# Decays of two groups of a quad in SBUF, the next decays in mid-step, and four smaller edits in a Mamba and convolution kernel

## The chip, the cores and the metric

The kernel runs on one core of one Trainium2 chip. The time is that of the device in microseconds (us), from the first to the last instruction and what lies around them; a kernel is measured several times and the median counts. A core has a matrix engine (TensorE, called PE), a vector engine (VectorE, DVE), an activation engine (ScalarE, ACT), a general engine (GpSimd, POOL) and a queue that issues transfers (SyncE, SP). Each takes its own instructions in the order in which they were written; semaphores tie the engines together. SBUF is the working memory; PSUM, eight banks of 128 x 512 float32, takes the results of matmuls, and POOL works in SBUF alone here.

## The reference

Four layers follow one another on x (8 images, 384 channels, 32 x 32 pixels, float32). Each normalises its input in 32 groups of channels and adds its result to it. Layer 0 is a Mamba block, layer 1 a spectral filter with a gated convolution, layer 2 a Mamba block with layer norm and an MLP, layer 3 a 3 x 3 depthwise convolution.

```python
def _mamba(xseq, ...):
    xin, z = jnp.split(xseq @ in_proj_w.T, 2, axis=-1)
    u = silu(conv1d_depthwise(xin, conv_w) + conv_b)
    dbc = u @ x_proj_w.T
    dt, Bm, Cm = dbc[..., :24], dbc[..., 24:40], dbc[..., 40:]
    dt = softplus(dt @ dt_proj_w.T + dt_proj_b)
    A = -jnp.exp(A_log)

    def step(h, inp):
        dt_t, B_t, C_t, u_t = inp
        dA = jnp.exp(dt_t[..., None] * A)
        h = dA * h + (dt_t * u_t)[..., None] * B_t[:, None, :]
        y = jnp.einsum('bdn,bn->bd', h, C_t)
        return (h, y)
    ...
    y = y + u * D
    return (y * silu(z)) @ out_proj_w.T
...
x = x + L0(_gn(x))
x = x + L1(_gn(x))
x = x + L2(_gn(x))
x = x + L3(_gn(x))
```

There are 768 inner channels with 16 states each, and 1024 positions in an image. The recurrence over positions, h = dA * h + dt*u*B, is the bulk of the work.

## The kernel before

**Tiling.** Each image is cut into two chunks of T = 512 positions, so 16 chunks of layer 0 and 16 of layer 2. A chunk's 768 channels times 16 states are 96 tiles of 128 rows by 512 positions. Four such tiles (groups 0 to 3) make a quad, and one quad is one step: 24 steps a chunk (6 blocks k of 128 channels, 4 quads `sub` in each), 768 steps in all. The recurrence is one DVE scan instruction per group.

**A step t of the main loop**, in the order in which its instructions are issued:

1. `times` of step t+1 (L623): POOL multiplies the four groups of g, which hold dt*u, by B, in two products of two groups each.
2. `scan` of step t (L643 to L660): for groups 0 and 1, DVE scans in place in the PSUM bank `dA[j]`, and multiplies by C into g (L654); for groups 2 and 3 the scan reads the bank and writes g, and POOL multiplies both by C in one product (L660). In the first chunk of an image the last column goes to `carry` (L653 from PSUM, L656 from SBUF).
3. Filler: up to 2 us of matmul work of other jobs (`jobs.step(t, 2.0)`).
4. `gather` of step t-1: matmuls that sum over states into the PSUM tile y; after the fourth quad of a block, u*D is added (a matmul by the diagonal matrix `w_D` in layer 0, a DVE instruction in layer 2) and DVE multiplies by the gate.
5. `begin` of step t+3: SP's transfer that spreads dt*u (`dud` in HBM) over g, after `jobs.until` has forced that chunk's `dud` to be there.
6. Filler: as much of other jobs as the room of this step allows (`jobs.step(t)`).
7. `decay` of step t+1: four matmuls put dt on the four banks `dA[0..3]`, and ACT takes exp(A * dt) of each in place.

PSUM's eight banks are the four `dA`, one y and three (`ps`) that all other work shares.

**Other work.** Everything else is a list of jobs, Python generators that go on piece by piece. `front` prepares the next chunk (normalise, project, convolve, u, then per block d `step_dt`: softplus into dt, POOL's dt*u into a tile du, four transfers of it to `dud`). `gates` makes the gate z of half a chunk; `measure` takes the statistics of a later image; `finish` does the output projection and, in layer 2, the MLP; `layer1` and `layer3` run once per image. Each has a first and a last step; the one due first goes first. `Jobs.step` lets a piece run when its matmul and vector costs fit the room left in this step (5.2 and 3.0 us in layer 0, 6.4 and 3.0 in layer 2). `Jobs.until(done)` is the exception: it runs pieces of all jobs, in order of due time, until a wanted thing is there. It is called at steps 4 and 16 of a chunk for the gates, and before `begin` for `dud`.

**SBUF tiles of the front.** The tag `spm` has two buffers, used by the softplus, by `measure`'s loads and by the layer norm's squares; `live["spm"]` says that `measure` holds them. `du` has two buffers, `dt` has seven (`NDT`).

Of the kernel before, what the change touches and what calls it, by code (L numbers as in the profile page):

```python
# [16 lines left out]
P = 128  # L17
# [72 lines left out]
class Jobs:  # L90
# [56 lines left out]

    def until(self, done):

        while not done():  # L150
            if not any(self.piece(job) for job in self.in_order()):
                raise RuntimeError("no job goes on")
# [3 lines left out]
def tile_conv_preact_d4(ctx: ExitStack, tc: tile.TileContext, a: dict, out: bass.AP):  # L156
# [9 lines left out]

    live = {"ps": 0, "dt": 0, "x": 0, "spm": False}
    work = [0.0, 0.0]
# [186 lines left out]

    def load_diagonal(w, pre):
        w["D"] = wk.tile([P, ND, P], F32, tag="w_D", name="w_D")
        nc.sync.dma_start(w["D"], a[pre + "D"].rearrange("d p q -> p d q"))

    def load_out(w, pre):  # L360
# [38 lines left out]
    def measure(s):  # L399

        blocks = [(h, k) for h in range(2) for k in range(KC)]
        loaded = {}

        def load(q):
            if q < len(blocks):
                h, k = blocks[q]
                x = loaded[h, k] = wk.tile([P, T], F32, tag="spm", name="xk", bufs=2)
                nc.sync.dma_start(
                    x, s["src"][s["b"], k * P : (k + 1) * P, h * T : (h + 1) * T]
                )  # L410

        live["spm"] = True
        load(0)
        load(1)
        yield NEXT

        def block(h, k):
            return loaded.pop((h, k)), lambda: load(blocks.index((h, k)) + 2)

        def all_read():  # L420
            live["spm"] = False

        s["stats"] = yield from group_stats(block, all_read, NEXT)
# [36 lines left out]
    def layer_norm(xn):  # L460
        ps = yield from ps_tile("ps_ln")
        for k in range(KC):
            mm(ps, ln_mean, xn[:, k, :], start=k == 0, stop=k == KC - 1)
        for k in range(KC):
            vector.tensor_sub(xn[:, k, :], xn[:, k, :], ps)
        ps_done()
        yield NEXT
        while live["spm"]:
            yield WAIT
        ps = yield from ps_tile("ps_lv")  # L470
        for k in range(KC):
            sq = wk.tile([P, T], F32, tag="spm", name="sq", bufs=2)
            act(sq, xn[:, k, :], AF.Square)
            mm(ps, ln_mean, sq, start=k == 0, stop=k == KC - 1)
        rsqrt(ps, ps, eps_ln)
        yield
        for k in range(KC):
            vector.scalar_tensor_tensor(
                xn[:, k, :], xn[:, k, :], ln_w[:, k : k + 1], ps, ALU.mult, ALU.mult
            )  # L480
        ps_done()
        yield NEXT
        for k in range(KC):
            act(xn[:, k, :], xn[:, k, :], AF.Identity, bias=ln_b[:, k : k + 1])
        yield NEXT

    def front(s):

        c, n = s["c"], s["n"]
        while n > 0 and ("gates", 1) not in chunks[n - 1]:  # L490
            yield WAIT
# [56 lines left out]
        exp_again()  # L548
        yield NEXT
        ps = yield from ps_tile("ps_x")  # L550
        for d in range(ND):
# [14 lines left out]
        def step_dt(d):  # L566
            got = {}


            def log(ps):  # L570
                mm(ps, w["dt"][DT0:RX, d * P : (d + 1) * P], dbc[DT0:RX, :])
                v = got["m"] = wk.tile([P, T], F32, tag="spm", name="spm", bufs=2)
                act(v, ps, AF.Abs)
                act(v, v, AF.Exp, scale=-1.0)
                act(v, v, AF.Ln, bias=1.0)

            def plus(ps):
                v = s["dt"][d] = wk.tile([P, T], F32, tag="dt", name="dt", bufs=NDT)
                vector.scalar_tensor_tensor(v, ps, 0.0, got["m"], ALU.max, ALU.add)

            def times_u(ps):
                v = got["du"] = wk.tile([P, T], F32, tag="du", name="du", bufs=2)
                nc.gpsimd.tensor_mul(v, s["dt"][d], u[d])

            def spill(ps):
                to = s["dud"][d] = dram.tile(
                    [NSUB * E8, 4, T], F32, tag="dud", name="dud", bufs=2 * ND
                )
                for j in range(4):
                    nc.sync.dma_start(to[:, j, :], got["du"][32 * j : 32 * (j + 1), :])  # L590

            return [both(log, plus), None, both(times_u, spill)]

        yield from pipe([("ps_bc", [spread(j)]) for j in range(2)])
        yield
        flying = []
        for d in range(ND):
            while live["dt"] >= NDT or live["spm"]:
                yield WAIT
            live["dt"] += 1  # L600

            flying.append(pipe([("ps_dt", step_dt(d))]))
            flying = [f for f in flying if next(f, f) is not f]
            yield NEXT
        while flying:
            flying = [f for f in flying if next(f, f) is not f]
            yield NEXT

# [18 lines left out]
    def decay(s, i):  # L627
# [4 lines left out]
        if sub == NSUB - 1:  # L632
            live["dt"] -= 1
        for j in range(4):
            act(dAs[j], dAs[j], AF.Exp, scale=s["w"]["A"][:, 4 * i + j : 4 * i + j + 1])

    def scan(s, i):
# [3 lines left out]
        for j in range(4):  # L641
            q = 4 * i + j
            nc.vector.tensor_tensor_scan(  # L643
                dAs[j] if j < own else g[:, j, :],
                dAs[j],
                g[:, j, :],
# [17 lines left out]
    def gather(s, i):  # L664
# [6 lines left out]
        for j in range(4):  # L671
            mm(y[32 * j : 32 * (j + 1), :], sely[:, sub, :], g[:, j, :], sub == 0, sub == NSUB - 1 and s["pre"] == "l2_")
        if sub == NSUB - 1:
            u = s["u"][k // NH][:, k % NH, :]
            if s["pre"] == "l0_":
                mm(y, s["w"]["D"][:, k, :], u, start=False)
            else:
                nc.vector.scalar_tensor_tensor(
                    y, u, s["w"]["vec"][:, k, 4:5], y, ALU.mult, ALU.add
                )  # L680
# [326 lines left out]
    jobs.until(lambda: ("gates", 0) in chunks[0])  # L1007
    load_diagonal(layer_w["l0_"], "l0_")
    jobs.until(lambda: not jobs.jobs)
# [3 lines left out]
    times(*steps[0])  # L1013
    decay(*steps[0])
    for t in range(total):
        s, i = steps[t]
        n = s["n"]
        later = chunks[n + 1] if n + 1 < len(chunks) else None
        if i == 0:
            jobs.add("gates", gates(s, 1), t + 1, t + 8)  # L1020
            if s["c"] == 0 and n + NCH < len(chunks):
                jobs.add("measure", measure(chunks[n + NCH]), t, t + NQ + 4)
            if later:
                jobs.add("front%d" % (later["pre"] == "l2_"), front(later), t + 3, t + 14)
                jobs.add("gates", gates(later, 0), t + 13, t + NQ + 2)
        if i % (NH * NSUB) == NSUB:
            jobs.until(lambda: ("gates", i // (NH * NSUB)) in s)
        if t + 1 < total:
# [10 lines left out]
        if t + AHEAD < total:  # L1039
            p, q = steps[t + AHEAD]  # L1040
            jobs.until(lambda: p.get("dud", {}).get(QUADS[q][0]))
            begin(p, q)
        jobs.step(t)
        if t + 1 < total:
            decay(*steps[t + 1])
    gather(*steps[-1])
# [132 lines left out]
```

## Time and profile before

| what | value |
|---|---|
| median of 3 runs | 7789.29 us (7782.02 to 7790.03) |
| the profiled execution | 7774.96 us, span 7773.2 us |
| granted TensorE clock, mean | 0.922 |
| first scan to first scan of layer 2 | 95.1 to 3552.3 us: 384 steps |
| first scan of layer 2 to POOL's last product | 3552.3 to about 7590 us: 384 steps |

A line of the profile's groups names the source line, engine and operation, then what is written and read with its shape and the count; behind the bar stand the busy time in us and the mean of one in ns, then the idle time of the engine just before these instructions and what ended most of it. Most calls go through helpers, so L177 is any matmul, L241 any activation and L85 most of DVE's work outside the scan; the names of the tiles tell them apart. In a table of waits a line reads: who waited, for whom, us in total, times, longest. In a table of stretches it reads: start and end, length, busy us of each engine with its instructions, granted clock, share of the DMA engines and GB/s. A timeline's line has the start, the length, the engine and the instruction; neighbours of one kind are merged into one line with their count.

### The profile page before, as it was taken

Reading aid. Unit: us, or ns where it says so; the run is one execution under the profiler, and the core shown is the slowest. Engines: PE = TensorE matmul, PEld = TensorE weight load, DVE = VectorE, ACT = ScalarE, POOL = GpSimd, SP = SyncE. Lnnn points to the kernel's source line nnn. Section 1 sums busy time; section 2 is a strip of 40 time slices with the busy share of each in tenths; the row PEclk is TensorE's granted clock in tenths of the full one; section 3 lists DMA queues with packets and bytes.
Section 4 is the critical chain, followed back from the end, with each engine's and each line's share of the span. In section 5 each row is a group of like instructions: output and inputs, shape, how many; then the busy total and the mean of one; then the engine's idle time right before and its main releaser. Section 6 shows DMA issues by size and latency. Waiting matters only on the chain. (4 is left out here: it accounts for less than half of the span.)

```text
span 7773.2 us, 76689 instructions
## 1 busy us (share of the span) xinstructions
PE 7244.1 (93%) x25762; PEld 3001.0 (39%) x25762; DVE 5787.0 (74%) x7350; ACT 4034.0 (52%) x6980; POOL 5638.8 (73%) x2710
## 2 busy tenths in 40 slices
PE   7989999999999999999999989999999999999998
PEld 2223333333333333333334434444444444444445
DVE  5988788888777878778746765767777677776871
ACT  4445555554554555455545544555555555555543
POOL 5888878788787878778646764767767677676770
PEclk8888889999888999988899999999999999999999
DMA  5666556556565646556536654666656666565662
GB/s 141 141 151 144 138 134 142 136 135 150 127 146 127 141 120 148 128 139 146 129 78 167 174 135 120 165 156 172 165 150 174 155 170 164 149 164 146 171 168 67
DMA packets 288919, 1122.50 MB, mean 144 GB/s; under 512 B 37386, under 2 KB 90970, under 8 KB 190220
## 3 DMA queue, kind: packets, MB, share of 16 engines
q1 hardware_dynamic: 288524, 1117.59, 58.4%
q8 instruction: 204, 3.34, 0.2%
q14 instruction: 191, 1.56, 0.1%
HBM read 1041.96 MB, written 75.50 MB: 144 GB/s over the span
## 5 line engine op out<-in xcount | busy, mean ns | idle before, releaser
L623 POOL TENSOR_TENSOR g<-g,bc 128x1024 f32<-128x1024 f32 x1536 | 3586.8, 2358 | 197.2 <-DMA g<-dud 181.2
L660 POOL TENSOR_TENSOR g<-g,bc 128x1024 f32<-128x1024 f32 x768 | 1806.2, 2352 | 1441.1 <-DVE carry L656 806.6
L241 ACT ACTIVATE dA<-dA,w_A 128x512 f32<-128x512 f32 x3072 | 1860.7, 662 | 1543.3 <-PE dA L177 1530.1
L177 PE MATMUL dA<-dt,selr 32*128 32x512 f32 x6144 | 1573.3, 677 | 70.6 <-DVE g L654 61.9
L643 DVE TENSOR_TENSOR_SCAN dA<-dA,carry,g 128x512 f32<-128x512 f32 x768 | 986.6, 1285 | 616.0 <-issue 275.6
L643 DVE TENSOR_TENSOR_SCAN dA<-dA,g 128x512 f32<-128x512 f32 x768 | 940.6, 1225 | 477.5 <-issue 167.7
L654 DVE TENSOR_TENSOR g<-dA,bc 128x512 f32<-128x512 f32 x1536 | 1053.9, 686 | 29.8 <-DVE dA L643 0.5
L177 PE MATMUL y<-g,sely 128*32 128x512 f32 x6144 | 934.1, 637 | 43.0 <-POOL g L660 37.5
L643 DVE TENSOR_TENSOR_SCAN g<-dA,carry,g 128x512 f32<-128x512 f32 x768 | 940.6, 1267 | 0.0
L643 DVE TENSOR_TENSOR_SCAN g<-dA,g 128x512 f32<-128x512 f32 x768 | 893.3, 1204 | 0.0
L177 PEld LDWEIGHTS dA<-dt,selr 32*128 32x128 f32 x6144 | 470.2, 191 | 984.4 <-DVE g L643 517.3
L177 PE MATMUL ps_dn<-h,mw 128*128 128x256 f32 x2304 | 573.9, 401 | 75.3 <-DMA mw<-in_l_mlp_w 58.6
L177 PE MATMUL ps_up<-t,mw 128*128 128x256 f32 x2304 | 566.8, 394 | 59.0 <-DMA mw<-in_l_mlp_w 44.2
L177 PE MATMUL ps_z<-xf,w_in 128*128 128x512 f32 x1152 | 586.1, 649 | 27.3 <-DVE dt L85 23.6
L177 PE MATMUL ps_in<-xf,w_in 128*128 128x512 f32 x1152 | 566.9, 633 | 27.3 <-DVE u L85 25.5
L177 PE MATMUL ps_dw<-tp,diag 96*96 96x512 f32 x1152 | 572.8, 638 | 15.2 <-ACT diag L241 15.2
L177 PE MATMUL ps_out<-u,w_out 128*128 128x512 f32 x1152 | 543.7, 619 | 10.2 <-DVE x L85 10.2
L177 PEld LDWEIGHTS ps_dn<-h,mw 128*128 128x128 f32 x2304 | 439.5, 197 | 277.0 <-issue 118.8
L177 PEld LDWEIGHTS ps_up<-t,mw 128*128 128x128 f32 x2304 | 425.8, 192 | 268.4 <-issue 148.9
L177 PE MATMUL ps_dw<-xp,diag 128*128 128x512 f32 x864 | 407.5, 622 | 42.2 <-ACT diag L241 40.9
L241 ACT ACTIVATE u<-ps_in,w_vec 128x512 f32<-128x512 f32 x192 | 149.4, 778 | 484.2 <-PE ps_in L177 484.2
L177 PEld LDWEIGHTS y<-g,sely 128*32 128x32 f32 x6144 | 134.2, 111 | 648.5 <-issue 461.1
(99 smaller groups left out, 6463.1 us busy)
## 6 DMA issues: line engine op xcount, KB each, us to landing
g<-dud SPq DMA_DIRECT2D x768, 1024.0 KB, 7.1
mw<-in_l_mlp_w SPq DMA_DIRECT2D x384, 384.0 KB, 7.4
dud<-du SPq DMA_DIRECT2D x768, 64.0 KB, 1.7
xk<-in_x SPq DMA_DIRECT2D x48, 256.0 KB, 4.2
xf<-in_x SPq DMA_DIRECT2D x16, 768.0 KB, 8.4
x<-in_x SPq DMA_DIRECT2D x16, 768.0 KB, 8.5
x_mid<-x SPq DMA_DIRECT2D x16, 768.0 KB, 4.6
xk<-x_mid SPq DMA_DIRECT2D x48, 256.0 KB, 5.0
```

What stands on the lines that cost most here:

```text
L177: nc.tensor.matmul(out_, lhsT, rhs, start=start, stop=stop)
L241: nc.scalar.activation(out_, in_, func, **kw)
L623: nc.gpsimd.tensor_mul(g, g, s["bc"][:, 0, :].unsqueeze(1).to_broadcast([P, 2, T]))
L643: nc.vector.tensor_tensor_scan(dAs[j] if j < own else g[:, j, :], dAs[j], g[:, j, :], 0.0 if s["c"] == 0 else carry[:, q : q + 1], ALU.mul ...
L654: nc.vector.tensor_mul(g[:, j, :], dAs[j], s["bc"][:, 1, :])
L660: nc.gpsimd.tensor_mul(g, g, s["bc"][:, 1, :].unsqueeze(1).to_broadcast([P, 4 - own, T]))
```

## The change

Six edits come together.

- The exponentials of groups 2 and 3 write SBUF tiles e2 and e3 (one buffer each) instead of their PSUM banks; scans 2 and 3 read them there. They are split off into `decay_out`.
- `decay` (four matmuls, two exponentials in place) is issued before the second filler; `decay_out` (two exponentials) stays behind it.
- dt*u is written over the softplus tile, so `du` goes; `spm` has three buffers. `live["spm"]` now names who holds them, and `front`'s loop over blocks waits for it, and goes on with blocks under way while the next one has to wait.
- The diagonal matrix of D is made by ACT from the identity, one block at a time, instead of being loaded whole.
- The layer norm's three squares are taken a piece ahead of their matmuls.
- `until` can be given a sort of job, which it then tries first; the gates of the two halves become two sorts, and those of the first half are due at step 20 instead of 26. Two further waits in `front` keep the order of buffers.

```diff
-    def until(self, done):
+    def until(self, done, kind=None):
         while not done():
-            if not any(self.piece(job) for job in self.in_order()):
+            late = [job for job in self.in_order() if job["kind"] == kind]
+            if not any(self.piece(job) for job in late + self.in_order()):
                 raise RuntimeError("no job goes on")
...
+        live["spm"] = "squares"
+        sq = [wk.tile([P, T], F32, tag="spm", name="sq", bufs=3) for _ in range(KC)]
+        for k in range(KC):
+            act(sq[k], xn[:, k, :], AF.Square)
+        yield NEXT
         ps = yield from ps_tile("ps_lv")
         for k in range(KC):
-            sq = wk.tile([P, T], F32, tag="spm", name="sq", bufs=2)
-            act(sq, xn[:, k, :], AF.Square)
-            mm(ps, ln_mean, sq, start=k == 0, stop=k == KC - 1)
+            mm(ps, ln_mean, sq[k], start=k == 0, stop=k == KC - 1)
+        live["spm"] = None
...
+        while n > 0 and "spread" not in chunks[n - 1]:
+            yield WAIT
         ps = yield from ps_tile("ps_x")
...
-                v = got["m"] = wk.tile([P, T], F32, tag="spm", name="spm", bufs=2)
+                v = got["m"] = wk.tile([P, T], F32, tag="spm", name="spm", bufs=3)
...
             def times_u(ps):
-                v = got["du"] = wk.tile([P, T], F32, tag="du", name="du", bufs=2)
-                nc.gpsimd.tensor_mul(v, s["dt"][d], u[d])
+                nc.gpsimd.tensor_mul(got["m"], s["dt"][d], u[d])
...
-        flying = []
-        for d in range(ND):
-            while live["dt"] >= NDT or live["spm"]:
-                yield WAIT
-            live["dt"] += 1
-            flying.append(pipe([("ps_dt", step_dt(d))]))
+        flying, d = [], 0
+        while d < ND or flying:
+            went = bool(flying)
+            if d < ND and live["dt"] < NDT and live["spm"] in (None, "dt"):
+                went = True
+                live["dt"] += 1
+                live["spm"] = "dt"
+                flying.append(pipe([("ps_dt", step_dt(d))]))
+                d += 1
             flying = [f for f in flying if next(f, f) is not f]
-            yield NEXT
-        while flying:
-            flying = [f for f in flying if next(f, f) is not f]
-            yield NEXT
+            if went and not flying:
+                live["spm"] = None
+            yield NEXT if went else WAIT
+        s["spread"] = True
...
-        for j in range(4):
+        for j in range(2):
             act(dAs[j], dAs[j], AF.Exp, scale=s["w"]["A"][:, 4 * i + j : 4 * i + j + 1])
+
+    def decay_out(s, i):
+        s["e"] = []
+        for j in range(2, 4):
+            e = wk.tile([P, T], F32, tag="e%d" % j, name="e%d" % j)
+            act(e, dAs[j], AF.Exp, scale=s["w"]["A"][:, 4 * i + j : 4 * i + j + 1])
+            s["e"].append(e)
...
                 dAs[j] if j < own else g[:, j, :],
-                dAs[j],
+                dAs[j] if j < 2 else s["e"][j - 2],
                 g[:, j, :],
...
+        if sub == NSUB - 2 and s["pre"] == "l0_":
+            s["D", k] = wk.tile([P, P], F32, tag="D", name="D")
+            act(s["D", k], eye, AF.Copy, scale=s["w"]["vec"][:, k, 4:5])
...
-                mm(y, s["w"]["D"][:, k, :], u, start=False)
+                mm(y, s.pop(("D", k)), u, start=False)
...
-                jobs.add("gates", gates(later, 0), t + 13, t + NQ + 2)
+                jobs.add("gates0", gates(later, 0), t + 13, t + NQ - 4)
         if i % (NH * NSUB) == NSUB:
-            jobs.until(lambda: ("gates", i // (NH * NSUB)) in s)
+            h = i // (NH * NSUB)
+            jobs.until(lambda: ("gates", h) in s, "gates%d" % h)
...
             begin(p, q)
+        if t + 1 < total:
+            decay(*steps[t + 1])
         jobs.step(t)
         if t + 1 < total:
-            decay(*steps[t + 1])
+            decay_out(*steps[t + 1])
```

More of the change, by code (lines that the diff above doesn't have):

```diff
@@ L165, in tile_conv_preact_d4 @@
     psy = ctx.enter_context(tc.tile_pool(name="psy", bufs=1, space=PSUM))
-    live = {"ps": 0, "dt": 0, "x": 0, "spm": False}
+    live = {"ps": 0, "dt": 0, "x": 0, "spm": None}
     work = [0.0, 0.0]
@@ L354, in load_mamba @@
         return w
-    def load_diagonal(w, pre):
-        w["D"] = wk.tile([P, ND, P], F32, tag="w_D", name="w_D")
-        nc.sync.dma_start(w["D"], a[pre + "D"].rearrange("d p q -> p d q"))
     def load_out(w, pre):
@@ L406, in load @@
                 h, k = blocks[q]
-                x = loaded[h, k] = wk.tile([P, T], F32, tag="spm", name="xk", bufs=2)
+                x = loaded[h, k] = wk.tile([P, T], F32, tag="spm", name="xk", bufs=3)
                 nc.sync.dma_start(
@@ L410, in load @@
                 )
-        live["spm"] = True
+        while live["spm"]:
+            yield WAIT
+        live["spm"] = "measure"
         load(0)
@@ L420, in all_read @@
         def all_read():
-            live["spm"] = False
+            live["spm"] = None
         s["stats"] = yield from group_stats(block, all_read, NEXT)
@@ L489, in front @@
         c, n = s["c"], s["n"]
-        while n > 0 and ("gates", 1) not in chunks[n - 1]:
+        while n > 0 and ("gates", 1) not in chunks[n - 1] or "stats" not in chunks[n - c]:
             yield WAIT
@@ L549, in front @@
         yield NEXT
+        while n > 0 and "spread" not in chunks[n - 1]:
+            yield WAIT
         ps = yield from ps_tile("ps_x")
@@ L589, in spill @@
                 for j in range(4):
-                    nc.sync.dma_start(to[:, j, :], got["du"][32 * j : 32 * (j + 1), :])
+                    nc.sync.dma_start(to[:, j, :], got["m"][32 * j : 32 * (j + 1), :])
             return [both(log, plus), None, both(times_u, spill)]
@@ L595, in front @@
         yield
-        flying = []
-        for d in range(ND):
-            while live["dt"] >= NDT or live["spm"]:
-                yield WAIT
-            live["dt"] += 1
-            flying.append(pipe([("ps_dt", step_dt(d))]))
+        flying, d = [], 0
[7 more added lines that the diff above has]
+                d += 1
             flying = [f for f in flying if next(f, f) is not f]
-            yield NEXT
-        while flying:
-            flying = [f for f in flying if next(f, f) is not f]
-            yield NEXT
+            if went and not flying:
+                live["spm"] = None
+            yield NEXT if went else WAIT
+        s["spread"] = True
     def begin(s, i):
@@ L1007, in tile_conv_preact_d4 @@
     jobs.until(lambda: ("gates", 0) in chunks[0])
-    load_diagonal(layer_w["l0_"], "l0_")
     jobs.until(lambda: not jobs.jobs)
@@ L1014, in tile_conv_preact_d4 @@
     decay(*steps[0])
+    decay_out(*steps[0])
     for t in range(total):
@@ L1019, in tile_conv_preact_d4 @@
         if i == 0:
-            jobs.add("gates", gates(s, 1), t + 1, t + 8)
+            jobs.add("gates1", gates(s, 1), t + 1, t + 8)
             if s["c"] == 0 and n + NCH < len(chunks):
@@ L1040, in tile_conv_preact_d4 @@
             p, q = steps[t + AHEAD]
-            jobs.until(lambda: p.get("dud", {}).get(QUADS[q][0]))
+            jobs.until(
+                lambda: p.get("dud", {}).get(QUADS[q][0]), "front%d" % (p["pre"] == "l2_")
+            )
             begin(p, q)
+        if t + 1 < total:
+            decay(*steps[t + 1])
         jobs.step(t)
         if t + 1 < total:
-            decay(*steps[t + 1])
+            decay_out(*steps[t + 1])
     gather(*steps[-1])
```

## The prediction, made before the changed kernel was run

> **What bounds the kernel now.** I read the page's engine shares and costliest groups first, then the waits, then the stretches, then two timelines. The groups that carry the argument, with the line of engine totals:
>
> ```profile
> PE 7244.1 (93%) x25762; PEld 3001.0 (39%) x25762; DVE 5787.0 (74%) x7350; ACT 4034.0 (52%) x6980; POOL 5638.8 (73%) x2710
> ...
> L623 POOL TENSOR_TENSOR g<-g,bc 128x1024 f32<-128x1024 f32 x1536 | 3586.8, 2358 | 197.2 <-DMA g<-dud 181.2
> L660 POOL TENSOR_TENSOR g<-g,bc 128x1024 f32<-128x1024 f32 x768 | 1806.2, 2352 | 1441.1 <-DVE carry L656 806.6
> ...
> L643 DVE TENSOR_TENSOR_SCAN g<-dA,carry,g 128x512 f32<-128x512 f32 x768 | 940.6, 1267 | 0.0
> L643 DVE TENSOR_TENSOR_SCAN g<-dA,g 128x512 f32<-128x512 f32 x768 | 893.3, 1204 | 0.0
> ```
>
> PE's 93% includes matmuls held back by waits, so I don't take it as a roof. Per step (768 of them), DVE is busy 5787.0/768 = 7.54 us and POOL 5638.8/768 = 7.34 us, in a step of about 9.8 us. No engine is full; the step is set by a loop through engines, which the waits show:
>
> ```profile
> ACT dA L241 <- PE dA L177: 1530.1, 847, 16.2
> ...
> PEld dA L177 <- DVE g L643: 517.3, 740, 1.7
> ...
> DVE dA L643 <- issue: 443.3, 237, 9.5
> DVE dA L643 <- ACT dA L241: 286.8, 129, 8.4
> ```
>
> PE waits for groups 2 and 3 of the last scan before it may refill their banks, ACT waits for PE, and DVE waits for ACT at the head of a step ("issue" there too: the first scan starts within a microsecond of the exponentials). This is what the change attacks. Its sum by stage (start, layer 0, layer 2, tail; PE, PEld, DVE, ACT, POOL busy):
>
> ```profile
> 0.00:95.00 95.00, 54.42 (x120) 23.36 (x120) 18.58 (x32) 36.65 (x56) 14.77 (x16) 0.83 0.47 134
> 95.00:3552.00 3457.00, 3265.38 (x10785) 1132.41 (x10786) 2839.33 (x3566) 1816.76 (x3220) 2814.61 (x1350) 0.90 0.58 138
> 3552.00:7590.00 4038.00, 3763.95 (x14345) 1744.64 (x14344) 2914.75 (x3727) 2123.17 (x3584) 2808.26 (x1342) 0.95 0.61 153
> 7590.00:7773.00 183.00, 160.37 (x515) 100.58 (x513) 14.38 (x26) 57.41 (x120) 1.13 (x5) 0.92 0.22 69
> ```
>
> So a step takes 3457/384 = 9.00 us in layer 0 and 4038/384 = 10.52 in layer 2, where POOL idles 4038 - 2808 = 1230 us, partly in bursts in which forced matmuls run and the scans stand still.
>
> The decisive lines are DVE's and POOL's timelines of one step:
>
> ```profile
> 274.77 2.33 DVE L643 TENSOR_TENSOR_SCAN g<-dA,g 128x512 f32<-128x512 f32 x2
> 277.13 2.36 DVE L656 COPY carry<-g 128x2 f32<-128x2 f32 x1
> ```
>
> ```profile
> 274.82 4.64 POOL L623 TENSOR_TENSOR g<-g,bc 128x1024 f32<-128x1024 f32 x2 [0.70 <-DMA g<-dud]
> 279.63 2.34 POOL L660 TENSOR_TENSOR g<-g,bc 128x1024 f32<-128x1024 f32 x1 [0.17 <-DVE carry L656]
> ```
>
> ```profile
> L656 DVE COPY carry<-g x384: 168/168/2359, 101.3 to 7367.5; 128x2 f32<-128x2 f32 x192
> ```
>
> The two g scans, which read the decay from PSUM, ran at full speed underneath a POOL multiplication. The copy after them, two elements from SBUF to SBUF, took 2.36 us instead of its median 0.168: it ended at 279.49, just behind POOL's product (274.82 + 4.64 = 279.46). [...]The longest one, 2359 ns, is one POOL product (2358).
>
> **What the skill says.** The Trainium skill, "SBUF — State Buffer", section "Who interferes with whom": DVE's second SBUF read port is GpSimd's only one; a DVE instruction with two SBUF inputs contends with a GpSimd instruction that reads SBUF, and whichever starts first holds the port for its whole length. The copy shows such a hold; no two-input DVE instruction of this kernel has both inputs in SBUF, so for a scan the trace is silent. "TensorE: Matmul & The Clock Gate", "Step-by-step: what each phase is for", says that matmuls stay in program order; the trace agrees (the dA loads waited 517.3 us for scans, with other matmuls queued behind).
>
> **The change part by part.**
>
> *Decays 2 and 3 into SBUF.* Two of the four exponentials per step write e2, e3 instead of their PSUM bank: same count, 594 ns for a PSUM-to-SBUF activation (z<-ps_z) against 662, nothing gained on an engine 52% busy. The wait of PE for the g scans (517.3 us) goes, since the bank is free after the exponential. But scans 2 and 3 now read e and g, both SBUF. If they take the shared port, they can no longer lie beside POOL. I counted from both timelines: 1044 of the 1834 us of g scans lie under an L623 product now, 606 of them in layer 0. The port then has to carry POOL's 7.34 plus (940.6 + 893.3)/768 = 2.39, together 9.73 us a step, against 9.00 in layer 0. By stage: layer 0 has 3457 - 2815 = 642 us of POOL idle and must place 384 x 2.39 = 918 us in it, 276 short; layer 2 has 1230 and must place 918, 312 over. Bounds: with no contention 0; with it and perfect packing 276 - 312 = -36; with every overlap added, +1044. I take contention.
>
> *Decays in mid-step.* Four matmuls and two exponentials move ahead of the second filler; the other two exponentials stay at the end. PE waits there for banks 0 and 1, free about 3.9 us into scan t (two scans of 1.28, two products of about 0.69), with gather(t-1) just ahead and the second filler queued behind. Counted from the end of scan t-1, product L660 ends at 2.35 and gather (1.06 in the timeline) at 3.4; bank 1 is free at about 1.1 (DVE's other work) + 3.9 = 5.0: up to 1.5 us of PE stall a step. DVE's wait for ACT (287 + 443 us) largely goes; late next is the port. decay_out waits for the scans of e2, e3 (one buffer each), and ACT's evictions of the next filler stand behind it; three PSUM banks cover that.
>
> *dt*u over the softplus tile.* The same 192 POOL products of 1272 ns, the same four spill DMAs on SP; the tile is held until the spill lands (1.7 us), and with three tiles it comes back three pieces, usually three steps, later: 0, a few us in forced stretches. *D by ScalarE:* 96 copies at 400 ns (as diag<-eye,vec) = 38 us of ACT beside 1817 busy of 3457; one 384 KB load less on SP: 0. *Squares ahead:* up to 71 + 40 us of PE wait for sq; PE off the limit, I take -20. *Work by its sort:* layer 2 now loses forced bursts such as
>
> ```profile
> 5719.34 2.37 POOL L660 TENSOR_TENSOR g<-g,bc 128x1024 f32<-128x1024 f32 x1 [28.46 <-DVE carry L656]
> ```
>
> There layer 3's matmuls (ps_dw) run before the gates that were wanted. Five of 28.5 and one of 61.7 us = 204 us of POOL idle can be filled; they are part of the 312 above. The burst at the turn (POOL idles of 70 and 49 us) runs work that the next front needs anyway: it stays, as does each front that comes late (80 us: 14.4, 21.7, 23.1, 20.7 at the ends of chunks 10, 12, 14, 16).
>
> **Sum.** Full port 9.73 x 768 = 7473; start and tail 95 + 183 = 278; so 7751. To it: the turn 119; late fronts 80; handovers, from the timeline above 0.03 (POOL to DVE) + 0.14 (DVE to POOL) + half of the carry copy's 0.17, so 0.255 x 768 = 196; PE late in layer 2, 0.15 a step as an estimate, 60 (bounds 0, if fillers are never late, and 250, some 0.65 a step, if nearly half of the 1.5 us stall shows); total 8206. The squares are within that. Layer 0 comes to about 10.1 us a step, layer 2 to about 10.6. The profiled execution took 7775 (span 7773), 14 under the median of 7789, so I say **8220 us**, 5.5% slower.
>
> **Rivals.**
> 1. *The scan doesn't hold the port* (the skill names tensor_tensor; and a scan takes 1204 ns for 512 elements where a product takes 686, so it may leave room). Then half of DVE's waits for decays, 730/2 = 365 us, go, a little more from the bursts, and PE's mid-step stall takes some back: about 7400. For it: 517 us of PE waiting as well. Against it: the copy. Faster.
> 2. *The port holds, but the freed order fills layer 2 almost to the floor*: late fronts vanish, PE costs nothing, half of the turn's idle is filled and half of the handovers hide: 7751 + 60 + 98 = 7909; from 7700 to 7950. For it: 204 us of bursts. Against: layer 0 cannot be under 9.73 a step.
> 3. *Port and PE order add up.* A DVE held at scan 2 also delays the evictions and products behind it; PE then waits at the mid-step decays with its filler behind. 1 us for half of the steps, 384 us more: 8600. For it: layer 2's PE is busiest. Decides if PE waits for DVE products rise above 1.5 us a step.
> 4. *The change doesn't do what it says*, the mid-step decays merely moving PE's wait from L643 to L654: contained in 3.
>
> **Chances.** Forecast 0.70 (7950 to 8450), rival 2 0.09, rival 3 with 4 0.05, rival 1 0.16 (7250 to 7700). Range 7600 to 8450: the forecast, rival 2 and the upper end of rival 1. A measurement here can tell 0.2%, some 16 us. Faster: rival 1 and the edge of 2, 0.17; same 0.03; slower 0.80.
>
> **What would show it.** Right: scans g<-e that stretch from 1.2 to as much as 3.6 us and end where an L623 or L660 ends; or POOL products whose start waits for them; POOL and stretched scans hardly overlapping; PE's wait on g scans gone; layer 0 near 10 us a step. Wrong: scans of 1.2 us under L623, layer 0 under 9.0 a step; then rival 1 holds. The bursts of 28.5 us should be gone in either case.

## The result and the profile after

The changed kernel takes 8496.3 us (median of 4 runs, 8492.63 to 8509.08) against 7785.66 us for the kernel before beside it: ratio 1.0917, 95% interval 1.0899 to 1.0936. The prediction said slower, rightly, but 5.5%, and 8496 lies above its range (7600 to 8450).

The costliest groups on the page of the changed kernel, with the line of engine totals (L630 and L675 are the POOL products that were L623 and L660, L658 is the scan):

```profile
PE 7355.9 (86%) x25762; PEld 3032.5 (36%) x25762; DVE 7340.8 (86%) x7350; ACT 4105.5 (48%) x7076; POOL 6093.1 (72%) x2710
...
L630 POOL TENSOR_TENSOR g<-g,bc 128x1024 f32<-128x1024 f32 x1536 | 4033.5, 2648 | 70.2 <-DMA g<-dud 63.6
L675 POOL TENSOR_TENSOR g<-g,bc 128x1024 f32<-128x1024 f32 x768 | 1809.0, 2355 | 1498.8 <-DVE g L658 752.0
...
L658 DVE TENSOR_TENSOR_SCAN g<-e,carry,g 128x512 f32<-128x512 f32 x768 | 1745.0, 2311 | 8.0 <-ACT e L242 7.9
L658 DVE TENSOR_TENSOR_SCAN g<-e,g 128x512 f32<-128x512 f32 x768 | 1710.5, 2266 | 6.1 <-ACT e L242 6.1
```

DVE has as many instructions as before and is busy 1554 us longer. The scans that read e take 2311 and 2266 ns instead of 1267 and 1204, 1536 scans of some 1.05 us more each; their own waits are 14 us in all. The time is inside the instruction. DVE's and POOL's timelines of one step in layer 0 show where:

```profile
2002.77 4.50 DVE L658 TENSOR_TENSOR_SCAN g<-e,carry,g 128x512 f32<-128x512 f32 x2
```

```profile
2000.53 5.66 POOL L630 TENSOR_TENSOR g<-g,bc 128x1024 f32<-128x1024 f32 x2
2007.41 2.34 POOL L675 TENSOR_TENSOR g<-g,bc 128x1024 f32<-128x1024 f32 x1 [1.22 <-DVE g L658]
```

Two products that took 4.68 us in the kernel before (at 2002 us of its trace) take 5.66, and the two scans 4.50 instead of 2.45 (at 2004 us there): product, scan, product, scan, one after the other.

The stretches (start, layer 0, layer 2, tail; columns as before):

```profile
0.00:89.00 89.00, 55.51 (x120) 23.55 (x120) 18.48 (x32) 36.96 (x56) 14.34 (x16) 0.85 0.45 132
89.00:4003.00 3914.00, 3277.09 (x10789) 1111.50 (x10790) 3690.14 (x3567) 1875.06 (x3318) 3073.48 (x1349) 0.88 0.51 122
4003.00:8281.00 4278.00, 3823.67 (x14211) 1772.10 (x14210) 3614.26 (x3720) 2118.35 (x3549) 3002.43 (x1343) 0.91 0.57 144
8281.00:8507.00 226.00, 199.61 (x645) 125.39 (x643) 17.92 (x32) 75.11 (x154) 2.84 (x5) 0.94 0.21 67
```

Layer 0 takes 3914/384 = 10.19 us a step, where 10.1 was predicted. Layer 2 takes 4278/384 = 11.14, where 10.6 was predicted, and the tail 226 instead of 183. So the miss is mostly in layer 2 and the tail. In layer 2 the bursts of 28.5 us at step 4 of even chunks have gone, but POOL's timeline at step 21 of such a chunk has this:

```profile
5907.36 0.20 POOL L545 TENSOR_TENSOR u<-u,hal 128x6 f32<-128x6 f32 x1 [16.47 <-DVE u L85]
5915.22 0.20 POOL L545 TENSOR_TENSOR u<-u,hal 128x6 f32<-128x6 f32 x1 [7.65 <-DVE u L85]
5931.85 1.28 POOL L587 TENSOR_TENSOR spm<-dt,u 128x512 f32<-128x512 f32 x1 [16.43 <-issue]
```

That is 40 us of idle POOL in front of one step, while PE does the next chunk's front in one piece (its projections, ps_in, stand there). Taking every gap of 15 us or more between POOL's products of g in layer 2, the kernel before has 204 us of them at step 4 of chunks 20, 22, 24, 26, 28 and 30, counting chunks from 0; the changed kernel has none there and 249 us at step 21 of the same chunks and of 21.

### The profile page after: what moved, and what is told of

It is laid out like the page before. It is cut to its first block, busy times and chain, and to the rows that moved or that the text cites. A ratio compares the mean times of both kernels' runs of the same rounds, so it can differ in the third digit from the quotient of the medians.

```text
span 8507.3 us, 77515 instructions
## 1 busy us (share of the span) xinstructions
PE 7355.9 (86%) x25762; PEld 3032.5 (36%) x25762; DVE 7340.8 (86%) x7350; ACT 4105.5 (48%) x7076; POOL 6093.1 (72%) x2710
## 4 chain that ended last, share of the span: by engine, by line
DVE 42%; PE 40%; ACT 6%; DMA 4%; issue 4%; POOL 2%; SPq 1%; DVEq 0%; POOLq 0%; ACTq 0%
DVE g L658 21%; DVE dA L658 11%; PE dA L178 6%; DVE g L669 5%; PE y L178 5%; PE ps_up L178 5%; PE ps_dw L178 4%; PE ps_dn L178 4%; PE ps_in L178 3%; PE ps_out L178 3%; PE ps_z L178 2%; PE ps_x L178 2%; DMA mw<-in_l_mlp_w 2%; POOL g L675 2%; PE ps_t L178 2%
## 5 line engine op out<-in xcount | busy, mean ns | idle before, releaser
L630 POOL TENSOR_TENSOR g<-g,bc 128x1024 f32<-128x1024 f32 x1536 | 4033.5, 2648 | 70.2 <-DMA g<-dud 63.6
L675 POOL TENSOR_TENSOR g<-g,bc 128x1024 f32<-128x1024 f32 x768 | 1809.0, 2355 | 1498.8 <-DVE g L658 752.0
L242 ACT ACTIVATE dA<-dA,w_A 128x512 f32<-128x512 f32 x1536 | 970.2, 658 | 2461.9 <-PE dA L178 2459.4
L658 DVE TENSOR_TENSOR_SCAN g<-e,carry,g 128x512 f32<-128x512 f32 x768 | 1745.0, 2311 | 8.0 <-ACT e L242 7.9
L658 DVE TENSOR_TENSOR_SCAN g<-e,g 128x512 f32<-128x512 f32 x768 | 1710.5, 2266 | 6.1 <-ACT e L242 6.1
L178 PE MATMUL dA<-dt,selr 32*128 32x512 f32 x6144 | 1337.9, 714 | 190.1 <-DVE g L669 188.7
L178 PE MATMUL y<-g,sely 128*32 128x512 f32 x6144 | 1164.9, 657 | 330.1 <-POOL g L675 276.8
L242 ACT ACTIVATE e<-dA,w_A 128x512 f32<-128x512 f32 x1536 | 1001.7, 687 | 345.7 <-DVE g L658 334.6
L658 DVE TENSOR_TENSOR_SCAN dA<-dA,carry,g 128x512 f32<-128x512 f32 x768 | 982.5, 1279 | 66.6 <-POOL g L675 25.3
L658 DVE TENSOR_TENSOR_SCAN dA<-dA,g 128x512 f32<-128x512 f32 x768 | 937.2, 1220 | 35.3 <-ACT dA L242 11.8
L178 PEld LDWEIGHTS dA<-dt,selr 32*128 32x128 f32 x6144 | 381.6, 202 | 1127.0 <-DVE g L669 682.6
L178 PEld LDWEIGHTS y<-g,sely 128*32 128x32 f32 x6144 | 164.0, 112 | 1089.4 <-POOL g L675 492.9
L85 DVE SCALAR_TENSOR_TENSOR u<-ps_in,w_vec,u 128x511 f32<-128x511 f32 (+1 forms) x384 | 284.6, 745 | 221.6 <-ACT u L242 134.8
## 6 DMA issues: line engine op xcount, KB each, us to landing
xk<-x_mid SPq DMA_DIRECT2D x48, 256.0 KB, 10.1
```

Source lines behind the costliest of these rows:

```text
L85: return call(out_, *args, **kw)
L178: nc.tensor.matmul(out_, lhsT, rhs, start=start, stop=stop)
L242: nc.scalar.activation(out_, in_, func, **kw)
L630: nc.gpsimd.tensor_mul(g, g, s["bc"][:, 0, :].unsqueeze(1).to_broadcast([P, 2, T]))
L658: nc.vector.tensor_tensor_scan(dAs[j] if j < own else g[:, j, :], dAs[j] if j < 2 else s["e"][j - 2], g[:, j, :], 0.0 if s["c"] == 0 else ...
L675: nc.gpsimd.tensor_mul(g, g, s["bc"][:, 1, :].unsqueeze(1).to_broadcast([P, 4 - own, T]))
```

## The experiments

Two theories from the start. P: a scan with two SBUF inputs and a POOL product can't run together. Q: they can, and the long scans only wait for something that the decays in mid-step delay. Later theories have letters too; each is stated in the expectation above its result. Each ratio below is against the kernel before, measured beside it (7780 to 7788 us).

**1. The disputed cost by itself.** A block of test instructions goes ahead of the kernel before.

```diff
+    def products():
+        for _ in range(4):
+            nc.gpsimd.tensor_mul(
+                gc[:, 0:2, :], gc[:, 0:2, :], gd[:, 0, :].unsqueeze(1).to_broadcast([P, 2, T])
+            )
+
+    def scans(x):
+        for j in (0, 1, 0, 1, 0, 1):
+            nc.vector.tensor_tensor_scan(
+                gb[:, j, :], x, ga[:, 2, :], 0.0, ALU.mult, ALU.add
+            )
...
+    products()
+    scans(dAs[0])
...
+    products()
+    scans(ga[:, 0, :])
```

> The kernel before with a block of test instructions put ahead of its work: six scans with both inputs in SBUF, six with one in PSUM, POOL products alone, then each kind of scan, and DVE products of two SBUF tiles, beside four POOL products. Theory P (a scan with two SBUF inputs and a POOL product can't run at the same time): alone 1.2 us for either scan; beside POOL the PSUM scans keep 1.2 us and POOL 2.36 us, while SBUF scans take 2.3 to 3.6 us or push POOL's products apart by the length of a scan; six scans and four products then take 6 x 1.2 + 4 x 2.35 = 16.6 us together instead of 9.4. Theory Q (they share the way finely, and the long scans in the changed kernel are only waits for something else): SBUF scans 1.2 to 1.5 us and POOL under 2.7 us, together under 11 us.

DVE's timeline of the block (the SBUF scans alone, PSUM scans beside POOL, SBUF scans beside POOL, eight products of two SBUF tiles beside POOL), and POOL's of the last three:

```profile
10.83 6.80 DVE L300 TENSOR_TENSOR_SCAN mb<-ma 128x512 f32<-128x512 f32 x6 [1.22 <-ACT ma L289]
...
37.19 6.80 DVE L300 TENSOR_TENSOR_SCAN mb<-dA,ma 128x512 f32<-128x512 f32 x6 [12.07 <-ACT ma L289]
48.64 15.20 DVE L300 TENSOR_TENSOR_SCAN mb<-ma 128x512 f32<-128x512 f32 x6 [4.65 <-ACT ma L289]
64.53 13.48 DVE L319 TENSOR_TENSOR mb<-ma 128x512 f32<-128x512 f32 x8 [0.70 <-ACT ma L289]
```

```profile
37.82 9.60 POOL L294 TENSOR_TENSOR mc<-mc,md 128x1024 f32<-128x1024 f32 x4 [1.84 <-ACT md L290]
...
49.27 12.38 POOL L294 TENSOR_TENSOR mc<-mc,md 128x1024 f32<-128x1024 f32 x4 [1.84 <-ACT md L290]
65.16 11.10 POOL L294 TENSOR_TENSOR mc<-mc,md 128x1024 f32<-128x1024 f32 x4 [3.52 <-ACT md L290]
```

The same six scans take 6.80 us alone, 6.80 from PSUM beside POOL, and 15.20 from SBUF beside POOL, and stretch POOL's four products from 9.60 to 12.38. P holds. Scan and product take turns, with a period of 3.22 us (single scans of 3.29 in the trace, overlapping a little). Scans alone start 1.12 us apart and products alone 2.42; if a scan's turn is 1.12 here too, a product's is 2.1, an estimate that fits 15.2 us, where the plain sum of both gave 16.6. The eight DVE products of two SBUF tiles are held in the same way: 2.82 us each beside POOL, 0.68 outside. This is what the Trainium skill says in "SBUF — State Buffer", "Who interferes with whom", of two SBUF inputs in general; here it is measured for a scan.

**2 to 4. The parts of the change undone, one at a time.** First the decays as before, with all other edits kept:

```diff
-            act(e, dAs[j], AF.Exp, scale=s["w"]["A"][:, 4 * i + j : 4 * i + j + 1])
+            act(dAs[j], dAs[j], AF.Exp, scale=s["w"]["A"][:, 4 * i + j : 4 * i + j + 1])
...
-                dAs[j] if j < 2 else s["e"][j - 2],
+                dAs[j],
...
-        if t + 1 < total:
-            decay(*steps[t + 1])
         jobs.step(t)
         if t + 1 < total:
+            decay(*steps[t + 1])
             decay_out(*steps[t + 1])
```

> The changed kernel with all four exponentials in place in PSUM and all four matmuls and exponentials at the end of the step again; the other edits stay. P and Q both: the scans are back at 1.2 us and the time within 100 us of the kernel before (7690 to 7890). If it stays above 8000, one of the other edits (sorting of the work, tiles of the softplus, squares, D) is what costs.

Measured: 7950 us, ratio 1.0209 (1.0186 to 1.0232), 60 us above what was expected. The scans are back (1205 and 1267 ns). So undoing the two edits of the decays takes away 546 of the 711 us, and 164 us stay with edits that I had put at nothing or at a gain.

Then the second half of that edit alone: decays at the end of the step, e still in SBUF.

> The changed kernel with the decay matmuls and the first two exponentials moved back to the end of the step; exponentials 2 and 3 still go to SBUF. P: the port is still shared, scans 2 and 3 still take over 2 us on average, time 8350 to 8700. Q (the place in mid-step is the cause, since PE then waits for DVE's products): 7750 to 7950, PE's waits of 683 + 189 us for the products of L669 gone and the scans back near 1.2 us.

Measured: 8506 us, 1.0921 (1.0897 to 1.0944), and the scans stay long (2087 and 2204 ns). Q falls: the place in mid-step is worth 10 us, no more than the spread of either kernel's runs, and the SBUF decays cost 556 (8506 less 7950). 441 of these are in layer 0, where a step goes from 8.97 to 10.12 us.

Then the old way of forcing jobs and the old due time:

```diff
-            late = [job for job in self.in_order() if job["kind"] == kind]
-            if not any(self.piece(job) for job in late + self.in_order()):
+            if not any(self.piece(job) for job in self.in_order()):
...
-                jobs.add("gates0", gates(later, 0), t + 13, t + NQ - 4)
+                jobs.add("gates0", gates(later, 0), t + 13, t + NQ + 2)
```

> The changed kernel in which a forced wait tries all late jobs by due time again and the first gates are due at step 26. Theory M (sorting only moved the burst: layer 3 no longer runs at step 4 of an even chunk of layer 2, so the front waits for it and is forced at step 21): the 40 us of idle at step 21 go, some 28 us at step 4 come back, time within 60 us of the changed kernel (8440 to 8560). Rival N (sorting itself is a gain, as predicted, and layer 2 is slow for the port alone): 100 to 250 us slower than the changed kernel.

Measured: 8430 us, 1.0822 (1.0795 to 1.085), 10 us below M's range, so sorting and the earlier due time together lose 67 us in this kernel; 45 of them are the tail, 181 us long here. The bursts of POOL idle are at step 4 again (24 us; 67 in chunk 20) and in those chunks gone from step 21. N falls; M is right about the bursts. Layer 2 as a whole, in the columns of the stretches above, is as long as in the changed kernel:

```profile
3968.10:8249.48 4281.38, 3789.64 (x14334) 1773.35 (x14334) 3502.61 (x3727) 2140.00 (x3577) 2981.02 (x1342) 0.93 0.57 145
```

The run doesn't price the sorting by itself, though: without it another loss appears in the odd chunks, half-done sums of layer 3, which runs 6 and 9 below explain. Five of them stand open for 120 us or more here, one in the changed kernel.

**5. POOL busy, but not reading.** Each product of times is replaced by three memsets of its tile; the factor B is left out, and so are the values of dt*u.

```diff
-            nc.gpsimd.tensor_mul(
-                g, g, s["bc"][:, 0, :].unsqueeze(1).to_broadcast([P, 2, T])
-            )
+            for _ in range(3):
+                nc.gpsimd.memset(g, 0.5)
```

> The changed kernel in which each POOL product of times (g by B) is replaced by three POOL memsets of the same tile, so that the factor B is left out and POOL is busy there (about 3 x 0.9 = 2.7 us for 2.35 in place of each product) but reads nothing. Theory P, with a port that only reads of POOL take: scans 2 and 3 beside these memsets are back at 1.2 us, and the time falls to 7700 to 8100. If any POOL work holds DVE up, they stay at 2 us or more and the time at 8400 or above.

Measured: 7972 us, once. The durations (minimum, median, maximum in ns) of the scans from e, first with memsets (2.9 us of POOL work for each product of 2.36), then in the changed kernel:

```profile
L657 DVE TENSOR_TENSOR_SCAN g<-e,g x768: 1191/1215/2433, 94.1 to 7513.8; 128x512 f32<-128x512 f32 x192
...
L657 DVE TENSOR_TENSOR_SCAN g<-e,carry,g x768: 1252/1275/2430, 313.7 to 7740.3; 128x512 f32<-128x512 f32 x192
```

```profile
L658 DVE TENSOR_TENSOR_SCAN g<-e,g x768: 1191/2085/3401, 93.4 to 8042.7; 128x512 f32<-128x512 f32 x192
...
L658 DVE TENSOR_TENSOR_SCAN g<-e,carry,g x768: 1250/2188/3462, 333.0 to 8279.3; 128x512 f32<-128x512 f32 x192
```

Nothing else was changed, and the median scan is at its own length again: it is POOL's reading that holds it up. 229 of the 1536 scans still take over 1.5 us; nearly all of these meet POOL's product by C (L674 in this kernel) or the one of dt*u, which stayed.

**6 to 8. What costs the other 164 us, and decays in mid-step without the port.** Run 6 is run 2 with the old jobs of run 4. Run 7 keeps everything in PSUM and puts groups 0 and 1 in mid-step, 2 and 3 at the end; run 8 is run 7 with the old jobs.

```diff
 def decay(s, i):
-        for j in range(4):
+        for j in range(2):
             rows = slice(32 * j, 32 * (j + 1))
             mm(dAs[j], selr[rows, sub, :], s["dt"][k][rows, :])
...
 def decay_out(s, i):
+        for j in range(2, 4):
+            rows = slice(32 * j, 32 * (j + 1))
+            mm(dAs[j], selr[rows, sub, :], s["dt"][k][rows, :])
```

> All decays in PSUM and at the end of the step, as before, and forced waits and due times as before; what stays of the change is D by ScalarE, dt*u over the softplus tile with its waits, and the squares. Theory M (the sorting and the earlier due time cost what the run with decays as before still lost, 164 us): 7760 to 7850. Rival R (the front's new waits and the shared softplus tiles cost it): 7880 to 7960.

Measured: 7993 us, 1.0258 (1.0237 to 1.0278), above the range of R too. M is wrong about the cost: with the old jobs the rest loses more, 208 us. Layer 0 is as before (9.07 us a step); the loss sits in the odd chunks of layer 2 (11.4 instead of 9.7).

> The changed kernel with all decays in PSUM, matmuls and exponentials of groups 0 and 1 in mid-step, those of groups 2 and 3 at the end of the step. Theory P: no port conflict, so scans of 1.2 us, and at least some of DVE's wait for ACT at the head of a step goes: 7750 to 7930, not above the run with all decays at the end (7950). Rival (mid-step decays cost PE its waits for DVE's products): 8000 to 8200.

> As the last, with forced waits and due times as before. A candidate for a version that beats both: if mid-step decays are a gain without the port, 7550 to 7750; if they only move PE's wait, 7780 to 7900.

Measured: 8200 us, 1.051 (1.0466 to 1.0554), and 8161 us, 1.0477 (1.0452 to 1.0501). P's expectation missed in run 7 and its rival was right; in run 8 both ranges missed. Without the port, decays in mid-step lose 250 us against run 2, and 168 us with the old jobs (run 8 against run 6). The waits of PE in run 2 (scans L655, products L666), then in run 7:

```profile
PEld dA L178 <- DVE g L655: 496.8, 716, 1.7
...
PEld dA L178 <- DVE g L666: 264.6, 203, 10.7
```

```profile
PEld dA L178 <- DVE g L670: 435.3, 381, 11.3
PEld dA L178 <- DVE g L659: 353.4, 446, 2.7
```

PE now stands twice in a step, in the middle for DVE's products (L670, 435 us instead of 265) and still at the end for the scans (L659, 353 instead of 497). The two waits together are only 27 us longer, so they don't account for the 250 us; 192 of these are in layer 0 (9.47 us a step instead of 8.97), and their cause isn't shown.

**9 to 11. The order of the other work.** In run 6, an odd chunk of layer 2 has these lines in PE's timeline:

```profile
5539.35 2.84 PE L177 MATMUL ps_dw<-xp,diag 128*128 128x512 f32 x6
...
5569.56 2.84 PE L177 MATMUL ps_in<-xf,w_in 128*128 128x512 f32 x6
...
5577.71 4.34 PE L177 MATMUL ps_in<-xf,w_in 128*128 128x512 f32 x6 [4.31 <-DVE u L85]
...
5592.29 5.46 PE L177 MATMUL ps_in<-xf,w_in 128*128 128x512 f32 x6 [3.83 <-DVE u L85]
...
5651.03 2.84 PE L177 MATMUL ps_dw<-xp,diag 128*128 128x512 f32 x6
```

Three of the nine taps of one layer 3 sum (six matmul instructions) run at 5539, the next three at 5651; for 112 us the sum holds one of the three shared PSUM banks, and an unfinished ps_up another for part of it. The front projects through what is left: each second ps_in waits 4 us until DVE has emptied the bank, and after such a wait the six matmuls take 4.3 to 5.5 us instead of 2.8; after waits of 1.5 us they take 2.81. "TensorE: Matmul & The Clock Gate", "Part 1: The HAM clock gate", says that PE's clock is cut to half after idle time and comes back with sustained work. The trace agrees: the granted clock is 0.50 over the six matmuls of 5.46 us and 1.00 over the six ps_in before them, which waited 1.5 us (from 5584.65 us). Run 9 takes out what moved the pieces: the extra piece of the squares.

```diff
-        live["spm"] = "squares"
-        sq = [wk.tile([P, T], F32, tag="spm", name="sq", bufs=3) for _ in range(KC)]
-        for k in range(KC):
-            act(sq[k], xn[:, k, :], AF.Square)
-        yield NEXT
         ps = yield from ps_tile("ps_lv")
         for k in range(KC):
-            mm(ps, ln_mean, sq[k], start=k == 0, stop=k == KC - 1)
-        live["spm"] = None
+            sq = wk.tile([P, T], F32, tag="spm", name="sq", bufs=3)
+            act(sq, xn[:, k, :], AF.Square)
+            mm(ps, ln_mean, sq, start=k == 0, stop=k == KC - 1)
```

> The run with all decays in PSUM at the end and the old forced waits (7993), with the layer norm's squares taken beside their matmuls again, one piece less in each front of layer 2. In the issue order the pieces of layer 2 then fall on the same steps as in the kernel before. Theory L (the extra piece shifts the others, so that a half-done depthwise sum of layer 3 holds a PSUM bank while the front projects; PE waits and its clock is cut): 7770 to 7830, TensorE's clock in odd chunks of layer 2 back to 0.97 or more. Rival R (the softplus tiles or the front's waits cost it): 7930 to 8010.

Measured: 7771 us, 0.998 (0.9966 to 0.9993). The same odd chunk, run 6 and then run 9 (the figure after POOL's busy time is the granted clock):

```profile
5475.00:5751.00 276.00, 226.84 (x869) 107.31 (x868) 181.44 (x198) 129.73 (x217) 183.26 (x87) 0.89 0.57 145
```

```profile
5424.00:5660.00 236.00, 215.57 (x909) 108.75 (x908) 180.50 (x198) 125.31 (x205) 177.65 (x85) 0.97 0.68 173
```

And a projection in mid-chunk of run 9, which waits 0.4 us:

```profile
5527.99 2.81 PE L177 MATMUL ps_in<-xf,w_in 128*128 128x512 f32 x6 [0.40 <-DVE u L85]
```

That edit costs 222 us (7993 against 7771), and D by ScalarE, dt*u over the softplus tile and the front's waits cost nothing, taken together. The edit removes a pause, and with it the flag that keeps `spm` for the squares; the loss is put down to the order of the pieces since the open sums go with it. Five of them stood open for some 125 us in the odd chunks of run 6, and none for more than 63 in run 9.

Run 10 puts the sorting of the gates alone into the kernel before: `until` as in the change and two sorts of gates, due times as before. (The change also lets the wait before `begin` try the front first; that stays out here.)

> The kernel before with nothing but the sorting: a forced wait tries its own sort of job first, due times as before. Theory M (it moves the bursts from step 4 to step 21 of even chunks of layer 2, with as much matmul work in them, and leaves more of layer 3 for the end): 7790 to 7900. The prediction's own view (204 us of idle filled): 7600 to 7720.

Measured: 8103 us, 1.0406 (1.0377 to 1.0436): worse than either side said. The front is forced at step 21, in odd chunks too (310 us of POOL gaps of 15 us or more, from chunk 20 on), and in five odd chunks a half-done sum of layer 3 stands open for some 132 us, from step 15 to the next chunk, over the front's projections; the granted clock in these chunks is 0.87. The tail is 220 us long. Run 11 leaves the jobs alone and widens what a step may take:

```diff
-ROOM = {"l0_": (5.2, 3.0), "turn": (6.4, 3.0), "l2_": (6.4, 3.0)}
+ROOM = {"l0_": (5.8, 3.0), "turn": (7.2, 3.0), "l2_": (7.2, 3.0)}
```

> The kernel before with nothing but more room for other work in a step: 5.8 us of matmuls instead of 5.2 in layer 0, 7.2 instead of 6.4 in layer 2. In the issue order nearly no forced matmul work is left (390 us of it before). Theory A (the bursts come from an allowance below what is to be done, not from which job is forced): 7500 to 7740. Rival (PE has no more to give in a normal step, and each step grows by what is put in): 7750 to 7950.

Measured: 7669 us, 0.9851 (0.9818 to 0.9885), faster than both kernels. With a little more room the same jobs hardly ever have to be forced: no gap of 15 us is left between POOL's products of g, of 418 us in the kernel before.

**12 to 16. The change with that room.** Run 12 is the changed kernel, 13 is run 2 and 14 is run 3, each with the room of run 11.

> The changed kernel with the same room. The forced front work at step 21 goes (about 230 us of idle in layer 2). If these bursts and the longer end are what the prediction missed, the time comes to what it said without them, 8150 to 8300; if the port alone and PE's waits make layer 2 slow, it stays at 8400 to 8520.

> The changed kernel with all decays in PSUM at the end of the step, and the wider room. Beside the changed kernel with that room (8123) it gives the cost of the SBUF decays where the order of the other work does nothing. Theory P: 7620 to 7720, so 400 to 500 us for the port, near the 9.73 us a step of the shared port less the 9.0 to 9.3 of this one. If the two come closer than 250 us, much of the 556 us found before was order too.

> The changed kernel with the decays at the end of the step, exponentials 2 and 3 into SBUF, and the wider room. Theory P: within 60 us of the changed kernel with that room (8123): the place of the decays is worth little where the port sets the step. If it is below 8000, mid-step decays cost by themselves.

Measured: 8123 us, 1.043 (1.04 to 1.0461); 7866, 1.0106 (1.0091 to 1.0121); 8271, 1.0623 (1.0605 to 1.0641). So the forced work and what goes with it cost the changed kernel 374 us (8496 less 8123, 27 us below the range expected). Layer 0 and layer 2 of run 12, in the columns of the stretches above:

```profile
90.00:3899.00 3809.00, 3274.29 (x10888) 1104.98 (x10889) 3658.40 (x3571) 1887.02 (x3371) 3049.49 (x1350) 0.89 0.53 126
3899.00:7960.00 4061.00, 3697.20 (x14291) 1751.36 (x14289) 3461.51 (x3725) 2115.49 (x3551) 2937.01 (x1341) 0.94 0.60 153
```

Layer 2 now takes 4061/384 = 10.58 us a step, as predicted, and 29 us of its POOL gaps are left. SBUF decays cost 405 us (8271 less 7866), 335 of them in layer 0; run 13 itself came out 150 us above what was expected. With the mid-step decays (run 12 against run 14) the time is 148 us shorter, where 60 at most was expected. The waits of run 14, then of run 12, show the exchange:

```profile
DVE dA L658 <- issue: 314.4, 133, 12.2
...
DVE dA L658 <- ACT dA L242: 278.6, 116, 10.9
PEld dA L178 <- DVE g L669: 259.3, 217, 10.6
```

```profile
PEld dA L178 <- DVE g L669: 680.5, 576, 10.9
...
DVE dA L658 <- issue: 59.4, 37, 6.3
DVE dA L658 <- ACT dA L242: 43.6, 33, 4.5
```

DVE's wait at the head of a step falls from 593 to 103 us, PE's for the products rises by 421. But the exchange isn't shown to pay. By stage, run 12 is 13 us longer than run 14 in layer 0 and 11 us longer in the even chunks of layer 2; only the odd chunks are shorter, by 173 us. There three sums of layer 3 stand open for over 100 us in run 14 and one in run 12, so the order of the other work has changed too, and the 148 us can't be put down to the mid-step itself. Runs 13 and 14 have three such sums each, which makes the 405 us the cleaner figure.

Two runs for the 197 us between runs 13 and 11: run 15 is run 9 with the wider room, run 16 is run 11 with the gates due at `t + NQ - 4`.

> All decays in PSUM at the end, old forced waits and due times, squares beside their matmuls, and the wider room: what stays of the change is D by ScalarE, dt*u over the softplus tile and the front's waits. If these are free, as predicted, it equals the kernel before with that room: 7640 to 7700. If they cost, 7750 or more.

> The kernel before with the wider room and nothing else but the first gates due at step 20 instead of 26. Theory L (the earlier gates go ahead of layer 3, whose half-done sums then hold a PSUM bank while the front projects): 7740 to 7870, most of what the changed kernel without its SBUF decays loses with this room (7866 against 7669). If the due time does nothing: 7640 to 7700.

Measured: 7668 us, 0.9857 (0.9829 to 0.9884), level with run 11; and 7899 us, 1.014 (1.0113 to 1.0168), 230 us slower than run 11 and 29 above L's range. The earlier due time is enough for the whole remainder, and PE's clock falls with it: 0.87 to 0.91 in three odd chunks, 0.96 in the same chunks of run 11. In the slowest of them a sum of layer 3 stands open for 185 us; what holds up the others isn't known.

## Why the prediction was right and where it was wrong

- *The port.* Right in kind: scan and POOL product take turns (run 1), and only POOL's reads matter (run 5). SBUF decays cost 556 us with the old room and 405 with the new (runs 2, 3, 13, 14), most of it in layer 0, as the sum had it. Rival 1, no contention, is refuted. That layer 0 also came out in size, 10.19 us a step for 10.1, is partly luck. In a quiet stretch of it (3600 to 3656 us) steps follow each other every 9.32 us, where the sum's terms (three products, two scans, the handovers) add up to 9.73, because the turns overlap a little; on the other side the late fronts left POOL gaps of 118 us there, 66 in the kernel before. And the carry copy that the prediction argued from reads only one SBUF tile, so it showed a hold by POOL but not this one; run 1 does.
- *Mid-step decays.* I had DVE's wait for ACT going and up to 1.5 us a step of PE stall coming, with the port hiding both. Both came: PE's waits for DVE's products are 871 us in the changed kernel, 1.13 us a step. The net is -10 us (run 3); the -148 us with little forced work (run 14) contain a change of order. Rival 3 is nearest in number (8600 for 8496), but its sign, PE waits above 1.5 us a step, didn't come. The variant tried in PSUM loses 250 us.
- *Work by its sort.* This is the step that failed: "layer 2 now loses forced bursts", "204 us of POOL idle can be filled". The sum has no forced work in layer 2 beyond the turn and one late front. The bursts left step 4, 204 us in all, and 249 us came at step 21, with 43 us more in the tail: their cause is an allowance a step below what there is to do (run 11), so what isn't forced early is forced late. I priced as a removal what was a move. With the wider room the gaps go, and layer 2 takes the 10.6 us a step predicted (run 12); that it hits this so closely is luck again, since the 10.6 contain the turn, which run 12 mostly hasn't.
- *Squares ahead.* Taken at -20. The extra pause shifted layer 3's pieces so that a half-done sum kept a PSUM bank; with the old jobs it cost 222 us (run 9). No run takes it out of the changed kernel, where one such sum, not five, stays open for over 100 us, so its share of the miss isn't known. The due time of the gates, which I didn't price at all, cost the kernel before 230 us by itself with the wider room (run 16).
- *D, the softplus tiles, the front's waits.* Put at 0, and 0: runs 9 and 15 equal the kernel before with the same room.
- *The sum.* 8206 was made for the span, 8507 came: layer 0 gives 0.09 x 384 = 35 of the 301 us, layer 2 0.54 x 384 = 207, the tail 43; the rest is rounding of the two rates and a start 6 us shorter. With the forced work taken away the changed kernel takes 8123 (run 12). The costs of single edits don't add up, since each also moves the other work: sorting the gates alone costs the kernel before 323 us (run 10), while sorting with the earlier due time gains 43 us with the squares ahead (runs 2 and 6).

What stays open is how much of layer 2's loss is clock and how much is wait, since the runs change both together, and what the mid-step decays are worth with the other work in the same order.

## What to carry to other kernels

Before moving a DVE operand from PSUM to SBUF, count the SBUF inputs of the instruction that reads it: with two, its time nearly adds to that of POOL's reading instructions (a pair of 1.2 and 2.34 us takes 3.22 in run 1), and a step can't be much shorter than the sum of both. An edit of a hand-written schedule that "only" reorders or pauses other work must be priced by where that work lands next and by the PSUM banks that half-done sums hold meanwhile. If work has to be forced, look at the allowance first: here 0.6 to 0.8 us more a step gained 1.5%, and no edit of the change is shown to gain anything over the kernel before.

## What was not expected of the hardware

- In run 1 a scan and a POOL product strictly alternate: with both queues full, neither got two turns in a row, and the records overlap (3.29 us a scan and 3.14 a product in a period of 3.22). The time spent waiting stands inside both durations, not in front of them.
- In run 6 waits of 4 us between groups of matmuls are enough for the next six to take up to 5.46 us instead of 2.81, at a granted clock of 0.50; waits of 1.5 us aren't. In a chunk with such waits the mean granted clock was 0.89 instead of 0.97.
